# Moving product casts, spills and stores to GpSimd, with four smaller moves, in a fused state-space convolution and gated feed-forward kernel

## The chip, the cores and the metric

The kernel runs on one core of a Trainium2 chip. The metric is the time of one execution on the device, in microseconds (us); lower is better. TensorE is the matmul engine (PE in a profile), VectorE is DVE, ScalarE is ACT, GpSimd is POOL, and SyncE (SP) issues most transfers. SBUF is the memory on the core, PSUM the memory that TensorE writes.

## The reference

The input x has 32 sequences of 64 channels by 1024 places. A convolution along the places comes first: for every channel a kernel of length 1024 is made from 64 complex exponentials, and the input, masked by each sequence's length, is convolved with it.

```python
K = 2.0 * jnp.einsum('hn,hnl->hl', Cs, jnp.exp(P)).real
y = jnp.fft.irfft(u_f * k_f, n=n)[..., :Lq]
y = y + u_m * D[:, None]
return y * mask[:, None, :]
```

Then a gated feed-forward runs over the 2048 rows (32 times 64) of width 1024, with an inner width of 2752. Its three weight matrices are packed in 4 bits, with a scale and a zero point for each group of 128 input rows. The result is added to x.

```python
gate = x2 @ Wg
up = x2 @ Wu
inter = gate * jax.nn.sigmoid(gate) * up
out = (inter @ Wd).astype(jnp.float16)
x = x + out.reshape(B, S, H)
```

## The kernel before, in words

**Convolution.** The 64 channels ("heads") are convolved by matmuls with Toeplitz matrices. A matrix is built by a load that reads the kernel row from device memory (kpad) with an overlapping pattern (`toeplitz`, L488; tiles named t, or borrowed space in w and ihl for the first heads). Each head takes eight steps of three matmuls, since matrix and input are each held as a high and a low half in float16 (`conv_head`, L505, matmuls L521). After two heads VectorE masks the result into y (L533), ScalarE casts its high half into xh (L536), and GpSimd subtracts to get the low half xl (L538). Sixteen heads make one block of 512 columns of the feed-forward's input. There are four blocks.

**Kernel rows.** They are made for eight heads at a time (four at the very start). `tables` (L419) and `factors` (L435) compute exponentials and phases on VectorE and ScalarE; `make_kernel` (L397) multiplies them on TensorE (L401, L403), splits the result (L406 on ScalarE, L407 on VectorE) and stores two halves to kpad (L409). The groups start at heads 0, 4, 8, 16, 24, 32, 40, 48 and 56. The groups of heads 16 and 24 are prepared in `kernel_8` (L841), which is started in the seventh step of the first block's convolution.

**Weights.** `unpack` (L546) loads packed bytes and zero points (z, from the pool "up"), shifts and masks on VectorE (L556), adds zero points on GpSimd (L562) and converts to 8-bit floats on VectorE (L566). There are 22 pieces for gate and up (qgu, qmix) and 8 for the down projection (qdn).

**Chains.** A chain is the sum over the groups of 128 input rows for one PSUM place. After each group the running sum is multiplied by the ratio of scales, on VectorE or ScalarE. The planner keeps one number for the balance, `lag`: work put on VectorE adds its cost, work on ScalarE subtracts, and `rescale` (L581) and `rescale_two` (L601) give the next rescaling to the engine that is behind. `gu_one` (L610) holds gate and up of one block in one chain. `gu_pair` (L632) takes two blocks in one chain: gate chains end in a Silu (L647, tile sg), up chains in the product v (L652). `products` (L589) splits v into two float16 halves: ScalarE casts (L595), GpSimd subtracts (L303, inside `pool_first`). The first block of a pair stays in SBUF (ihl), the second goes through the tile "spill" (one buffer) to device memory (L599). v has one buffer too. `dn_pair` (L667) is the down projection: 22 groups per chain (L677, L678, L680), a residual load (xr, in the two buffers that sg uses), a cast (L696), an addition (L697) and a store (L698). For every second block it loads the spilled products back into ihl (L685).

**Order of work.** The list `items` runs eight stages: 0 and 1 are single chains, four each; 2 is the gate and up pairs of blocks 0 and 1; 3 and 4 the down projection of these blocks; 5 the pairs of blocks 2 and 3; 6 and 7 their down projection. `roll` (L709) goes round the active chains: three in PSUM place "b", and a fourth in place "a" in the stages named wide (1, 2, 5, 6, 7). Beside the chains run side generators at rates: in stage 0 the unpacking and `second` (convolution of block 1), in stages 1 and 2 the unpacking, in stage 2 also `third` (groups 32 and 40), in stages 3 and 4 `fourth` (groups 48 and 56) and `convs` (blocks 2 and 3). RATES holds steps per round. A framework then orders each engine's instructions by priority; `after` and `mark` keep an instruction behind a marked one. Each engine, and each engine's queue of transfers, runs its instructions in order, so a transfer that waits holds up those behind it.

## Time and profile before

| What | us |
|---|---|
| Median of 3 runs (1094.53 to 1096.8) | 1096.46 |
| The profiled execution | 1098.36 |
| Its span, first to last instruction | 1096.1 |
| TensorE busy | 1029.1 |
| VectorE busy | 789.6 |
| ScalarE busy | 775.9 |
| GpSimd busy | 219.3 |
| First convolution matmul | 24.7 |
| First single chain (stage 0) | 66.5 |
| First pair chain (stage 2) | 145.8 |
| First down chain (stage 3) | 412.6 |
| Last convolution matmul | 603.6 |

Busy time of TensorE counts modelled ends of pipelined matmuls. A row of instruction groups gives the line, the engine, the operation, the tiles written and read, the count, busy time and mean, and the idle time before it with what ended it. TensorE's clock can be lowered for a time; the row PEclk gives the granted share.

### The profile page before, as it was taken

How to read it: one execution, taken by the hardware profiler on the slowest of the kernel's cores; microseconds unless marked ns; L12 is line 12 of the kernel's file. 1: busy time of each engine (PE TensorE's matmuls, PEld its weight loads, DVE VectorE, ACT ScalarE, POOL GpSimd, SP SyncE). 2: the span in 40 equal slices, each digit the busy share in tenths (PEclk: the TensorE clock that was granted, in tenths of full speed). 3: DMA queues.
4: the chain of work that ended last, by engine and by line, in shares of the span. 5: the costliest groups of instructions: out<-in, count | busy, mean ns of one | idle time of the engine just before them, and what ended most of it. 6: DMA issues, size and time to landing. Idle time of an engine off the chain costs nothing.

```text
span 1096.1 us, 15375 instructions
## 1 busy us (share of the span) xinstructions
PE 1029.1 (94%) x5834; PEld 515.6 (47%) x5834; DVE 789.6 (72%) x903; ACT 775.9 (71%) x1024; POOL 219.3 (20%) x215
## 2 busy tenths in 40 slices
PE   3889989899999999998998999999999999999996
PEld 3757534344344444554556444444444444444442
DVE  8975578888986667875663767766676667777776
ACT  5636678888887677774663777677777776777775
POOL 0332233443431121113004002111111111002001
PEclk9989999999999999999998999999999999999998
DMA  6866223233200202336665001000000000424202
GB/s 199 288 212 199 85 76 123 83 112 102 73 20 20 79 21 97 130 102 224 211 192 193 1 29 68 20 20 20 20 20 20 20 20 20 144 77 136 86 1 77
DMA packets 55169, 99.73 MB, mean 91 GB/s; under 512 B 9396, under 2 KB 10292, under 8 KB 55096
## 3 DMA queue, kind: packets, MB, share of 16 engines
q1 hardware_dynamic: 54520, 98.73, 27.6%
q8 instruction: 45, 0.74, 0.3%
q14 instruction: 28, 0.23, 0.1%
q10 hardware_dynamic: 576, 0.03, 0.0%
HBM read 78.99 MB, written 19.76 MB: 90 GB/s over the span
## 4 chain that ended last, share of the span: by engine, by line
PE 76%; DVE 9%; DMA 5%; ACT 4%; issue 4%; POOL 1%; SPq 0%; ACTq 0%; DVEq 0%; POOLq 0%
PE chq L639 21%; PE chq L640 20%; PE chq L677 12%; PE chq L678 12%; PE cq L521 6%; PE chq L618 2%; PE chq L619 2%; DMA t<-kpad 2%; DVE chq L584 2%; ACT chq L608 1%; DMA kpad<-kb 1%; DVE chq L604 1%; ACT chq L587 1%; DVE w L566 1%; DVE v L652 1%
## 5 line engine op out<-in xcount | busy, mean ns | idle before, releaser
L639 PE MATMUL chq<-xh,w 128*128 128x512 f16 x1216 | 457.6, 379 | 15.0 <-DVE v L652 8.0
L640 PE MATMUL chq<-xl,w 128*128 128x512 f16 x1216 | 456.0, 379 | 0.0
L587 ACT ACTIVATE chq<-chq,gur 128x1024 f32<-128x1024 f32 x312 | 332.4, 1087 | 106.1 <-PE chq L640 104.9
L584 DVE TENSOR_SCALAR chq<-chq,gur 128x1024 f32<-128x1024 f32 x234 | 299.9, 1290 | 117.9 <-PE chq L640 115.7
L608 ACT ACTIVATE chq<-chq,dnr 128x512 f32<-128x512 f32 x336 | 220.7, 661 | 91.6 <-PE chq L678 86.3
L604 DVE TENSOR_TENSOR chq<-chq,dnr 128x1024 f32<-128x1024 f32 x168 | 206.4, 1232 | 95.7 <-PE chq L678 92.0
L677 PE MATMUL chq<-ihl,wd 128*128 128x512 f16 x672 | 255.1, 380 | 6.9 <-DMA ihl<-spill 2.8
L678 PE MATMUL chq<-ihl,wd 128*128 128x512 f16 x672 | 254.9, 380 | 0.0
L640 PEld LDWEIGHTS <-w 128*128 128x128 fp8e4 x1216 | 118.7, 98 | 163.0 <-issue 26.2
L639 PEld LDWEIGHTS <-w 128*128 128x128 fp8e4 x1216 | 118.7, 98 | 146.5 <-POOL spill L303 2.5
L303 POOL TENSOR_TENSOR ihl<-v,ihl 128x512 f16<-128x512 f32 x42 | 48.9, 1165 | 401.4 <-ACT ihl L595 401.4
L521 PEld LDWEIGHTS <-t 128*128 128x128 f16 x1152 | 85.8, 100 | 44.7 <-DMA t<-kpad 10.2
L678 PEld LDWEIGHTS <-wd 128*128 128x128 fp8e4 x672 | 65.8, 98 | 72.7 <-issue 8.6
L521 PE MATMUL cq<-uh,t 128*128 128x64 f16 (+7 forms) x720 | 93.4, 230 | 6.5 <-DMA t<-kpad 6.2
L677 PEld LDWEIGHTS <-wd 128*128 128x128 fp8e4 x672 | 65.8, 98 | 70.9 <-DMA ihl<-spill 2.9
L538 POOL TENSOR_TENSOR xl<-y,xh 128x512 f16<-128x512 f32 x28 | 34.5, 1235 | 213.8 <-ACT xh L536 178.7
L521 PE MATMUL cq<-ul,t 128*128 128x256 f16 (+3 forms) x360 | 74.3, 230 | 0.1
L652 DVE SCALAR_TENSOR_TENSOR v<-chq,gul,sg 128x1024 f32<-128x1024 f32 x38 | 48.6, 1278 | 15.3 <-PE chq L640 10.4
L608 ACT ACTIVATE chq<-chq,gur 128x512 f32<-128x512 f32 x62 | 40.9, 661 | 20.6 <-PE chq L619 19.6
L618 PE MATMUL chq<-xh,w 128*128 128x512 f16 x128 | 49.2, 390 | 4.2 <-ACT xh L536 3.2
L303 POOL TENSOR_TENSOR spill<-v,spill 128x512 f16<-128x512 f32 x42 | 49.3, 1174 | 8.6 <-ACT spill L595 8.6
L619 PE MATMUL chq<-xl,w 128*128 128x512 f16 x128 | 49.1, 390 | 0.0
(242 smaller groups left out, 721.8 us busy)
## 6 DMA issues: line engine op xcount, KB each, us to landing
t<-kpad SPq DMA_DIRECT2D x48, 512.0 KB, 4.8
spill<-spill SPq DMA_DIRECT2D x42, 256.0 KB, 2.0
ihl<-spill SPq DMA_DIRECT2D x42, 256.0 KB, 2.9
u<-xF SPq DMA_DIRECT2D x12, 512.0 KB, 4.2
xr<-xT SPq DMA_DIRECT2D x12, 512.0 KB, 4.5
out<-xr SPq DMA_DIRECT2D x24, 256.0 KB, 2.6
w<-qgu SPq DMA_DIRECT2D x21, 256.0 KB, 3.9
z<-zc SPq DMA_DIRECT2D x21, 256.0 KB, 3.6
```

The source lines that it names most:

```text
L303: self.nc.gpsimd.tensor_tensor(out, a, b, op)
L521: nc.tensor.matmul(q[:, d:, h % 2, :], t0[:, lw, 128 * d:128 * d + 128], uu[:, 0:8 - d, h % 4, :], start=(d == 0 and k == 0 and h % 2 == 0 ...
L584: self.mark("dve", self.nc.vector.tensor_scalar(q, q, col, None, ALU.mult))
L587: self.mark("act", self.nc.scalar.activation(q, q, AF.Copy, scale=col))
L604: self.mark("dve", self.nc.vector.tensor_tensor(q, q, cols.to_broadcast([128, 2, 512]), ALU.mult))
L608: self.mark("act", self.nc.scalar.activation(q[:, k], q[:, k], AF.Copy, scale=cols[:, k]))
L618: nc.tensor.matmul(q[:, k], lw, xh[:, g, :], start=(g == 0), stop=False, skip_group_check=True)
L619: nc.tensor.matmul(q[:, k], lw, xl[:, g, :], start=False, stop=(g == GH - 1), skip_group_check=True)
L639: nc.tensor.matmul(q[:, b], lw, xh[:, g, :], start=(g == 0), stop=False, skip_group_check=True)
L640: nc.tensor.matmul(q[:, b], lw, xl[:, g, :], start=False, stop=(g == GH - 1), skip_group_check=True)
L677: nc.tensor.matmul(q[:, j], lw, self.ihl[:, g, 0], start=(g == 0), stop=False, skip_group_check=True)
L678: nc.tensor.matmul(q[:, j], lw, self.ihl[:, g, 1], start=False, stop=False, skip_group_check=True)
```

## The change

The same matmuls are issued before and after. What moves:

- Both halves of the product v are made on GpSimd: the 84 casts of L595 become GpSimd copies (`pool_copy`). The planner no longer counts them as ScalarE work.
- GpSimd issues the 42 spills and the 24 output stores of blocks 0 to 2, which SyncE issued.
- The stores of kernel rows for heads under 32 go through ScalarE's queue (before: under 8), six more.
- The conversions of the first three gate and up pieces, two each, run on ScalarE.
- Tables and factors of the group of heads 24 to 31, the fourth group of eight, move from the first convolution into `second`, beside the first chains, and are held behind marked work.
- Unpacking has four z buffers in place of three; down weights come in three pieces per matrix (8, 8 and 6 groups) in place of two of 11.
- From head 32 on, inputs and Toeplitz matrices may be loaded across the border of a block.
- Rates change, and `fourth` steps once for each call where it took two.

```diff
-RATES = {"first": (0.1, 5.0), "second": 0.5, "pairs": 0.45, "third": 0.25,
-         "fourth": 0.9, "convs": 1.6}
+RATES = {"first": (0.1, 5.6), "second": 0.5, "pairs": 0.47, "third": 0.2,
+         "fourth": 1.0, "convs": 1.9}
...
-        self.up = self.up_stack.enter_context(tc.tile_pool(name="up", bufs=3, side="right"))
+        self.up = self.up_stack.enter_context(tc.tile_pool(name="up", bufs=4, side="right"))
...
+    def pool_copy(self, out, a):
+        with self.tc.high_priority(offset=300):
+            self.nc.gpsimd.tensor_copy(out, a)
...
-            (nc.scalar if h0 < 8 else nc.sync).dma_start(
+            (nc.scalar if h0 < 32 else nc.sync).dma_start(
...
-        held = h0 >= 32
+        held = h0 >= 24
...
-                with self.after("dve" if h0 >= 32 else None):
+                with self.after("dve" if h0 >= 24 else None):
...
-            if k // 4 not in self.us and k // 16 == hh // 16:
+            if k // 4 not in self.us and k < 64 and (k // 16 == hh // 16 or hh >= 32):
...
-            if k not in self.t0 and k // 16 == hh // 16 and k in self.known:
+            if k not in self.t0 and (k // 16 == hh // 16 or hh >= 32) and k in self.known:
...
-            with self.after("dve"):
-                nc.vector.tensor_scalar(dst[:, a:b], raw[:, a:b], -64.0, None, ALU.add, saturate=False)
-            self.dve(150 + (b - a) / 2)
+            if act:
+                with self.after("act"):
+                    nc.scalar.activation(dst[:, a:b], raw[:, a:b], AF.Identity, bias=self.cst[:, 108:109], saturate=False)
+            else:
+                with self.after("dve"):
+                    nc.vector.tensor_scalar(dst[:, a:b], raw[:, a:b], -64.0, None, ALU.add, saturate=False)
+                self.dve(150 + (b - a) / 2)
...
-        nc.scalar.copy(hl[:, 0], v)
-        self.act(520)
+        self.pool_copy(hl[:, 0], v)
         self.pool_first(hl[:, 1], v, hl[:, 0], ALU.subtract)
         if b == 1:
-            nc.sync.dma_start(self.spill[i], hl)
+            nc.gpsimd.dma_start(self.spill[i], hl)
...
-            nc.sync.dma_start(self.io["out"][128 * n:128 * n + 128, 512 * blk:512 * blk + 512], xr[:, j])
+            (nc.gpsimd if blk < 3 else nc.sync).dma_start(self.io["out"][128 * n:128 * n + 128, 512 * blk:512 * blk + 512], xr[:, j])
...
-        for k, h0 in ((2, 16), (3, 24)):
-            every(c.tables(kg, h0, 8))
-            every(c.factors(kg, h0, 8, xd[k]))
+        every(c.tables(kg, 16, 8))
+        every(c.factors(kg, 16, 8, xd[2]))
...
-        for _ in range(12):
+        yield from c.tables(kg, 24, 8)
+        for _ in range(3):
+            yield
+        yield from c.factors(kg, 24, 8, xd[3])
+        for _ in range(4):
             yield
         c.make_kernel(kg, 24, 8, "a")
...
-    fourth_it = slowly(fourth(), 2)
+    fourth_it = slowly(fourth(), 1)
```

The rest of the diff gives the down weights and their zero points the layout of the three pieces, and a column of constants for the conversions on ScalarE.

## The prediction

> **What bounds the kernel now.** I read the page first: shares, the forty slices, the chain.
>
> ```profile
> span 1096.1 us, 15375 instructions
> PE 1029.1 (94%) x5834; PEld 515.6 (47%) x5834; DVE 789.6 (72%) x903; ACT 775.9 (71%) x1024; POOL 219.3 (20%) x215
> PEclk9989999999999999999998999999999999999998
> DMA  6866223233200202336665001000000000424202
> PE 76%; DVE 9%; DMA 5%; ACT 4%; issue 4%; POOL 1%; SPq 0%; ACTq 0%; DVEq 0%; POOLq 0%
> ```
>
> TensorE is most of the chain, and the last half of the slices has full clock and little DMA: what can be won lies before slice 23 (620 us). Its 94% is no share of its peak: ends are modelled. So I priced a matmul where nothing interrupts it and compared stretches with that, by the busy time in chosen windows (engine busy time with instruction counts, granted clock, DMA share, GB/s).
>
> ```profile
> 62.00:66.50 4.50, 1.24 (x18) 0.81 (x19) 3.80 (x7) 1.28 (x3) 3.41 (x5) 0.80 0.39 129
> 66.50:72.00 5.50, 5.50 (x15) 1.97 (x15) 2.70 (x5) 1.55 (x3) 0.19 (x1) 0.54 1.00 299
> 118.00:145.80 27.80, 27.75 (x128) 12.20 (x126) 21.43 (x23) 22.14 (x35) 4.51 (x6) 1.00 0.05 19
> 173.00:310.00 137.00, 125.39 (x564) 54.79 (x563) 120.46 (x187) 115.60 (x125) 59.28 (x65) 1.00 0.30 96
> 310.00:412.00 102.00, 101.42 (x491) 45.51 (x490) 73.09 (x68) 74.92 (x82) 18.81 (x17) 1.00 0.10 32
> 588.00:595.00 7.00, 2.97 (x31) 2.08 (x32) 0.69 (x1) 0.62 (x1) 3.17 (x3) 0.91 0.79 253
> 595.00:604.00 9.00, 9.00 (x98) 8.12 (x97) 0.94 (x2) 0.62 (x1) 1.16 (x1) 0.69 0.32 113
> 604.00:945.00 341.00, 340.93 (x1572) 153.43 (x1571) 240.22 (x191) 247.80 (x276) 52.16 (x46) 1.00 0.07 26
> ```
>
> From 118 to 145.8 us, 128 matmuls of 512 columns take 27.8 us: 0.217 us each. From 604 to 945 it is 341/1572 = 0.217 again, with both vector engines idle 30% of the time. That stretch and the 139 us after it are TensorE alone; no edit to another engine can shorten them. From 173 to 310, 564 x 0.217 = 122.4 us of 137: 14.6 us lost, with VectorE 88% and ScalarE 84% busy. Around 62 and 588 the clock is low and TensorE waits. The chain of waits, and the SyncE queue by time, say why at 588:
>
> ```profile
> 578.95 3.46 DMA out<-xr
> 582.95 4.96 DMA t<-kpad
> 587.95 1.36 PE cq L521 x15
> 589.31 5.19 DMA t<-kpad
> 594.55 9.10 PE cq L521 x96
> ```
> ```profile
> 585.22 4.04 SPq L698 DMA_DIRECT2D out<-xr  x4
> 589.31 8.69 SPq L499 DMA_DIRECT2D t<-kpad  x4
> ```
>
> The four stores of the output hold SyncE from 585.22 to 589.26, each until its POOL addition is done, and the load of the next convolution matrix stands behind them.
>
> **What the skill says.** The Trainium skill, GPSIMD Engine Reference, section 4.1, has GpSimd about half as fast as VectorE with two inputs and "1-input is roughly line-rate"; section 3.1 gives 2.6 cycles an element for two. The trace agrees on two: the subtraction of L303 (128x512) takes 1165 ns. DMA: Bandwidth & Descriptors, "Latency and other measured facts", prices the first byte of a GpSimd transfer at 1 us against 0.6 us for SyncE or ScalarE, and its anatomy section has 2.0 us plus bytes/436 GB/s; no run here has a GpSimd transfer. SBUF — State Buffer, "Who interferes with whom": two-port VectorE modes lock GpSimd out, and GpSimd's descriptors with it. The unpacking conversion L566 averages 829 ns, with single ones from 0.63 to 1.65 us, as such a lock would make it. TensorE: Matmul & The Clock Gate, Part 1: after a pause the array runs at half rate until it has been busy about 3.4 us. The trace agrees: after the gap at 62 us matmuls start 0.43 us apart until 71.5.
>
> **The change, part by part.** Sums are against the profiled run (span 1096.1, run 1098.36), in us saved.
>
> (a) Both product parts on POOL. ScalarE loses 84 casts (L595, 612 to 616 ns), 51.6 us; POOL gains 84 copies. Bounds of a copy: 0.44 us (512 elements at line rate, an estimate from the page) and 1.17 us (the two-input row); I take 0.75, so 63 us, which lies in POOL's 80% idle time. Only what falls in 173 to 310 is worth time: nine pairs end there, 18 x 0.614 = 11.1 us less for ScalarE, and the planner's lag spreads it over both engines. Divided by two: 5.5. Bounds 0 (TensorE's own waits stay) and 11 (all is critical). After 310 ScalarE's idle time covers it. Against it: POOL now holds v longer. By the timeline v is held 3.0 us from the end of L652 to the last subtraction, and free for 3.1 us before the next close pair, from 310 on for 0.8 to 3.7. With POOL: 2 x 0.75 + 2 x 1.165 = 3.8, plus up to 1 of a transfer's issue ahead of it. What queues behind the late L652 is VectorE's rescaling and, on TensorE, the chain that wants that PSUM place: -1 (0 to -4; the copies at 1.17 make 4.7).
>
> (b) Spills and output stores on POOL: 66 transfers, each 1 us of issue (estimate from the page; 0.4, SyncE's issue, to 2.6), 66 us of POOL time behind its own results. SyncE loses 66 waits, 440.5 us behind L303 and some 100 behind the additions. The stage's end gains: the longest wait for t<-kpad, 4.5, plus half rate afterwards: 96 matmuls took 9.1 where two heads at 53.5 us (48 in 3.22) make it 6.4, so 2.7. Together 7.2; I take 6.5, since these loads still wait for their three buffers (4 to 7.2). At 508 the load ihl<-spill was issued behind two stores: TensorE waited 2.8, then eight starts 0.43 apart lost 1.7; 4.5, of which I take 3.5 (0 to 4.5). Spill of the second block's single chains, 147.8 to 151.9: lands 4.04 after issue; POOL's would need 2.6 (estimate, 256 KB): 1 (-1 to 2).
>
> (c) h0 < 32 stores of kernel rows on ScalarE: six issues of 0.3 to 0.7 us leave SyncE, where group 8's last was issued at 34.47, group 16's at 63.60 behind a u load waiting until 61.46. TensorE waits 3.0 at 44.76; VectorE's half is ready only at 33.74, so the issue moves 0.7, and the landing (6.2) shortens as it leaves the row of 512 KB loads: 2 (0 to 3). On ScalarE the second issue waits for VectorE ahead of a y cast; nobody waits for that cast there.
>
> (d) First three conversions on ScalarE (6 of 1.13 us, estimate from ScalarE: Activation LUTs, "What ACT_TABLE_LOAD costs", 0.28 us + 0.833 ns an element; VectorE loses 6 x 0.83 to 1.2), and group 24's tables and factors (some 13 VectorE operations, 6.5 to 7 us) out of the first convolution. VectorE is 100% busy from 50 to 62 and TensorE waits for L533 there: 1.69 + 0.49 = 2.2 saved (0 to 2.2). At the end of that convolution, group 16's half row L407 ran at 63.17 in the old order; in the new one it stands before the last two y, and the next convolution's first matmuls come ahead of the first chain. Old: 61.5 to 72.4 for 16 matmuls and a kernel group (4.4 of work), 6.5 lost. New: the load lands an estimated 2 to 4 after the end, plus 2 of half rate: 2.5 saved (0 to 5).
>
> (e) Group 24 within the first chains: its 7 us meet VectorE at 16.3 of 30 busy (82 to 112). The new TensorE order puts 88 conv and 36 chain matmuls, 13 us plus the cold start, ahead of it; the VectorE chain up to e1 is about 20 us: costs 0 to 2. Waits there of 0.8 (L566) and 2.0 (t<-kpad at 116) ease: net 1.5 (-2 to 2.8).
>
> (f) Early loads across convolution blocks, four z buffers, rates, dn pieces in three (four more L556, about 2 us of VectorE in its fullest stretch): the loads are in (b); -2 for the pieces and for waits in new places that I can't name (-6 to +1).
>
> Sum: 5.5 - 1 + 6.5 + 3.5 + 1 + 2 + 2.2 + 2.5 + 1.5 - 2 = 21.7. The profiled run becomes 1098.4 - 21.7 = 1076.7. The median of the runs shown is 1.9 under the profiled one: 1075. Every low end together is 9 lost, every high end 39 saved; neither is likely.
>
> **Rivals.**
>
> Queue only (0.20): POOL's longer hold eats what ScalarE gives up. For it: L652 already ends 8.0 us of TensorE's waits at L639. Then the 5.5 goes, and half of (c) to (e), 4.1: 12 saved, 1084.
>
> All waits (0.13): the 14.6 lost to 310 mostly vanish, since both engines drop below the point at which TensorE waits: 33 saved, 1063. Against it: 236 of 274 us of engine time falls only to about 226.
>
> No change (0.04): new waits match the gains; 1096.
>
> Slower (0.13): POOL becomes the pace. Copies at 1.17, a transfer's issue at 2.6, one unpack piece at 0.75 and a lock of 0.8 ahead give a hold of 2.3 + 2.3 + 2.6 + 0.75 + 0.8 = 8.8 against 6.1 free. 2.7 us late at all 17 pairs before 430 is 46; if three quarters reach TensorE, 34 against 22 saved: 1108. It decides from a hold of about 7.8, where 17 x 1.7 x 0.75 meets the 22. Against it: VectorE's PSUM rescales show no two-port speed (1290 ns for 1024), so most POOL work would run unlocked.
>
> **How the numbers follow.** Main case 0.50, 1066 to 1084. 80% range: leave out most of the slower case, the no-change case's upper half and the tail under 1062: 1062 to 1094. Faster 0.50 + 0.20 + 0.13 = 0.83; same (within 0.2%, about 2 us, as fine as this kernel can be measured) 0.04; slower 0.13.
>
> **What would show it.** Right: no gap over 2 us before L521 near 590 and full clock after it; VectorE and ScalarE both under 85% in the pairs before 310; L533 no longer ending waits near 60. POOL near 350 us busy. Wrong: L652 waiting on POOL; waits of L521 for t<-kpad at the first chains; TensorE waiting for group 24's e1; copies over 1.2 us.

## The result: no change that can be measured

The changed kernel takes 1097.07 us (median of 20 runs, 1093.66 to 1100.91), the kernel before 1095.99 us (20 runs, 1094.52 to 1097.66) in the same comparison. The ratio is 1.001, with a 95% interval of 1.0 to 1.0019. The prediction had 1075 and 83% for faster: it was wrong. Of its cases it is the one given 0.04, in which new waits match the gains.

The page of the profile after, the lines that answer to those shown of before:

```profile
span 1096.3 us, 15389 instructions
PE 1026.1 (94%) x5834; PEld 512.9 (47%) x5834; DVE 764.4 (70%) x879; ACT 761.8 (69%) x969; POOL 304.9 (28%) x365
...
PEclk9989999998999999999999999999999999999998
DMA  6866223222200201335754101000000000424202
...
PE 72%; DVE 8%; POOL 3%; DMA 3%; ACT 2%; issue 2%; SPq 0%; DVEq 0%; POOLq 0%; ACTq 0%
```

VectorE and ScalarE gave up 25 and 14 us, 39 together where 51.6 us of casts alone left ScalarE, and GpSimd took 86. The span is the same, and GpSimd is 3% of the chain where it was 1%. The same eight windows as before (busy us and instruction counts of TensorE, its weight loads, VectorE, ScalarE and GpSimd, then granted clock, DMA share, GB/s) say where time went:

```profile
62.00:66.50 4.50, 2.77 (x12) 1.64 (x12) 0.00 (x0) 0.00 (x0) 0.00 (x0) 0.50 1.01 315
66.50:72.00 5.50, 5.50 (x36) 2.85 (x35) 4.40 (x8) 3.06 (x5) 0.00 (x0) 0.82 0.70 259
118.00:145.80 27.80, 26.90 (x124) 12.00 (x123) 19.62 (x19) 21.73 (x34) 8.55 (x10) 1.00 0.08 25
173.00:310.00 137.00, 122.03 (x534) 52.87 (x532) 111.27 (x164) 104.08 (x102) 68.24 (x87) 0.96 0.26 87
310.00:412.00 102.00, 98.08 (x472) 43.90 (x472) 76.96 (x80) 70.76 (x74) 33.83 (x41) 1.00 0.11 35
588.00:595.00 7.00, 7.00 (x60) 4.33 (x59) 4.36 (x5) 4.75 (x8) 3.66 (x4) 1.00 0.37 116
595.00:604.00 9.00, 9.00 (x91) 6.17 (x89) 5.79 (x6) 4.26 (x7) 5.36 (x7) 1.00 0.53 184
604.00:945.00 341.00, 340.41 (x1575) 153.64 (x1574) 227.93 (x180) 239.19 (x246) 93.45 (x117) 1.00 0.08 29
```

Two rows carry the result. At 588 to 604 TensorE now works without a gap and at full clock (before: 2.97 us busy of the first 7, clock 0.91 and 0.69). From 173 to 310 it issues 534 matmuls where it issued 564: 30 x 0.217 us = 6.5 us lost, although VectorE fell from 120.5 to 111.3 us and ScalarE from 115.6 to 104.1. From 310 to 412 it is 19 matmuls, 4.1 us. Not all of the loss is waiting: from 173 to 310 the granted clock is 0.96 where it was 1.00.

By the first matmul of each kind in the timelines, the stages stand as follows (us; "pair stage" is from here on the stage of blocks 0 and 1, from the first pair chain to the first down chain, and "stretch" is the time from that down chain to the last convolution matmul):

| | before | after |
|---|---|---|
| first single chain | 66.5 | 64.7 |
| first pair chain | 145.8 | 143.0 |
| first down chain | 412.6 | 421.1 |
| last convolution matmul | 603.5 | 603.4 |
| pair stage | 266.8 | 278.1 |
| stretch | 190.9 | 182.3 |

The pair stage lost 11.3 us, the stretch won 8.6, and 2.8 were ahead at the start. Each of the first two is made of idle time of TensorE and of time at a lowered clock. In the pair stage the idle time went from 15.1 to 21.2 us, and the clock, full throughout before the change, was at half (granted share 0.50) for 13.7 us (from 147.0 for 3.4, from 211.8 for 3.4, from 246.0 for 6.8). TensorE was busy for 11.7 of these 13.7 us, so by an estimate from these figures the half clock cost about 5.9 us, as much as the added idle time. In the stretch the idle time went from 11.4 to 8.1 us and the half clock from 10.2 to 3.4. The view of waits (what TensorE waited for: us in all, times, longest), from 140 to 425 us, names the loss. Before:

```profile
PE chq L639 <- DVE v L652: 8.0, 7, 1.8
```

After (L650 is the old L639, L663 the old L652):

```profile
PE chq L650 <- DVE v L663: 15.6, 6, 5.5
```

A new chain waits for its PSUM place until VectorE has made the product v from what stands there. The longest such wait ends at 212.42; the next ones end at 247.27 and 311.88. As gaps, that is as time between the starts of two matmuls beyond the length of one at full rate, they are 5.7, 5.0 and 3.0 us, and the experiments speak of gaps in this sense. The first two are where the clock fell to half at 211.8 and 246.0. TensorE's timeline there (start, us, what, and in brackets the idle time before it and what ended it):

```profile
206.52 0.38 PE L651 MATMUL chq<-xl,w 128*128 128x512 f16 x1
212.42 0.59 PE L650 MATMUL chq<-xh,w 128*128 128x512 f16 x1 [5.51 <-DVE v L663]
```

VectorE's timeline between this product and the one before it:

```profile
200.16 1.27 DVE L663 SCALAR_TENSOR_TENSOR v<-chq,gul,sg 128x1024 f32<-128x1024 f32 x1
...
203.02 1.44 DVE L562 TENSOR_SCALAR w<-w,cst 128x1024 uint16<-128x1024 uint16 x1
204.38 1.17 DVE L91 SCALAR_TENSOR_TENSOR t<-t 128x64 f32<-128x64 f32 x1
205.47 0.96 DVE L562 TENSOR_SCALAR w<-w,cst 128x1024 uint16<-128x1024 uint16 x1
206.36 2.75 DVE L91 SCALAR_TENSOR_TENSOR t<-t 128x64 f32<-128x64 f32 x2
209.03 0.68 DVE L576 TENSOR_SCALAR w<-w 128x1024 fp8e4<-128x1024 uint8 x1
209.63 0.47 DVE L91 SCALAR_TENSOR_TENSOR t<-t 128x64 f32<-128x64 f32 x2
...
211.09 1.27 DVE L663 SCALAR_TENSOR_TENSOR v<-chq,gul,sg 128x1024 f32<-128x1024 f32 x1
```

And GpSimd's in the same time:

```profile
201.50 1.00 POOL L309 CAST ihl<-v 128x512 f16<-128x512 f32 x1 [3.39 <-DVE v L663]
202.45 0.61 POOL L309 CAST spill<-v 128x512 f16<-128x512 f32 x1
203.02 1.15 POOL L305 TENSOR_TENSOR ihl<-v,ihl 128x512 f16<-128x512 f32 x1
204.14 1.33 POOL L305 TENSOR_TENSOR spill<-v,spill 128x512 f16<-128x512 f32 x1
205.43 0.72 POOL L568 TENSOR_TENSOR w<-w,z 128x256 int32<-128x256 int32 x1
206.10 0.56 POOL L610 DMA_DIRECT2D spill<-spill  x1
206.68 2.08 POOL L568 TENSOR_TENSOR w<-w,z 128x256 int32<-128x256 int32 x3
```

GpSimd works without a break from 201.50 to 208.76: two copies, two subtractions, the issue of the spill, four unpack additions. VectorE, meanwhile, does not wait for data; its instructions take long. The small L91 on 64 elements, 0.22 us when GpSimd is still (209.63, two in 0.47), takes 1.17 and then 2.49 (the first of the two at 206.36; it ends 0.09 us after GpSimd's last addition). The shift L562, 0.47 undisturbed, takes 1.44 and 0.96. The Silu that the product needs was done at 205.40; the product started at 211.09, because all of this stands ahead of it in VectorE's order. Over 150 to 410 us VectorE's instructions took 31.0 us more than their undisturbed lengths (an estimate, with the tenth percentile of each operation and shape for undisturbed); before the change it was 19.7. The rescaling L596, which reads and writes PSUM, is not stretched: it takes 1291 ns on average, before it took 1290.

At 63 us, a new wait stands where old ones were (TensorE, 30 to 70 us): 4.4 us for a load ahead of the first chain, which the prediction had listed as a sign against it. The two waits for L533 that step d was to end, 1.69 us at 58.4 and 0.49 at 62.1, are gone. In all, TensorE's waits from the first convolution matmul to the first pair chain add up to 11.9 us where they were 13.2: most of them moved. Those for loads:

```profile
PE cq L527 <- DMA t<-kpad: 7.1, 2, 4.4
```

SyncE's queue near 590 (SPq rows: start, us in the queue, how many) no longer holds a store; two loads of the convolution matrix still wait there for 4.92 us, but TensorE has other matmuls meanwhile. The wait near 510 did not go: for 2.8 us at 511.9 before (`ihl<-spill`) there are now two for the same load, 2.0 at 520.7 and 2.3 at 531.3. The queue:

```profile
584.15 4.28 SPq L696 DMA_DIRECT2D ihl<-spill  x2
589.12 4.92 SPq L505 DMA_DIRECT2D t<-kpad  x2
```

### The profile page after: what moved, and what is told of

It is laid out like the page before. It is cut to its first block, busy times and chain, and to the rows that moved or that the text cites. A ratio compares the mean times of both kernels' runs of the same rounds, so it can differ in the third digit from the quotient of the medians.

```text
span 1096.3 us, 15389 instructions
## 1 busy us (share of the span) xinstructions
PE 1026.1 (94%) x5834; PEld 512.9 (47%) x5834; DVE 764.4 (70%) x879; ACT 761.8 (69%) x969; POOL 304.9 (28%) x365
## 4 chain that ended last, share of the span: by engine, by line
PE 72%; DVE 8%; POOL 3%; DMA 3%; ACT 2%; issue 2%; SPq 0%; DVEq 0%; POOLq 0%; ACTq 0%
PE chq L650 21%; PE chq L651 20%; PE chq L688 12%; PE chq L689 12%; PE cq L527 4%; DVE chq L596 2%; PE chq L629 1%; PE chq L630 1%; DVE v L663 1%; POOL w L568 1%; DMA out<-xr 1%; ACT chq L619 1%; POOL spill L305 1%; DMA spill<-spill 1%; ACT sg L658 1%
## 5 line engine op out<-in xcount | busy, mean ns | idle before, releaser
L650 PE MATMUL chq<-xh,w 128*128 128x512 f16 x1216 | 462.7, 382 | 21.2 <-DVE v L663 15.6
L651 PE MATMUL chq<-xl,w 128*128 128x512 f16 x1216 | 461.5, 382 | 0.6 <-DVE xl L544 0.6
L599 ACT ACTIVATE chq<-chq,gur 128x1024 f32<-128x1024 f32 x333 | 353.2, 1086 | 147.7 <-PE chq L651 147.1
L596 DVE TENSOR_SCALAR chq<-chq,gur 128x1024 f32<-128x1024 f32 x213 | 273.6, 1291 | 135.1 <-PE chq L651 130.7
L650 PEld LDWEIGHTS <-w 128*128 128x128 fp8e4 x1216 | 119.3, 98 | 145.6 <-issue 3.7
L309 POOL CAST ihl<-v 128x512 f16<-128x512 f32 x42 | 28.0, 666 | 332.1 <-DVE v L663 250.8
L527 PE MATMUL cq<-uh,t 128*128 128x64 f16 (+6 forms) x720 | 92.9, 227 | 6.0 <-DMA t<-kpad 6.0
L663 DVE SCALAR_TENSOR_TENSOR v<-chq,gul,sg 128x1024 f32<-128x1024 f32 x38 | 48.5, 1277 | 17.6 <-PE chq L651 13.0
L658 ACT ACTIVATE sg<-chq,gul 128x1024 f32<-128x1024 f32 x38 | 42.3, 1112 | 11.9 <-PE chq L651 11.8
L708 POOL TENSOR_TENSOR xr<-xr,o 128x512 f32<-128x512 f32 x24 | 28.4, 1186 | 79.3 <-ACT o L707 78.1
L629 PE MATMUL chq<-xh,w 128*128 128x512 f16 x128 | 49.4, 389 | 0.2 <-ACT chq L619 0.2
```

What stands on the lines that cost most here:

```text
L527: nc.tensor.matmul(q[:, d:, h % 2, :], t0[:, lw, 128 * d:128 * d + 128], uu[:, 0:8 - d, h % 4, :], start=(d == 0 and k == 0 and h % 2 == 0 ...
L596: self.mark("dve", self.nc.vector.tensor_scalar(q, q, col, None, ALU.mult))
L599: self.mark("act", self.nc.scalar.activation(q, q, AF.Copy, scale=col))
L629: nc.tensor.matmul(q[:, k], lw, xh[:, g, :], start=(g == 0), stop=False, skip_group_check=True)
L650: nc.tensor.matmul(q[:, b], lw, xh[:, g, :], start=(g == 0), stop=False, skip_group_check=True)
L651: nc.tensor.matmul(q[:, b], lw, xl[:, g, :], start=False, stop=(g == GH - 1), skip_group_check=True)
```

## The experiments

All times are medians; a ratio is against the kernel before, measured on the same chip, with its 95% interval. The sets were measured on different chips, where the kernel before had medians of 1095.99 to 1097.2 us, so a difference between medians of two sets carries about 1 us of this; the ratios don't. Pair stage, stretch and waits are of the one profiled execution of each kernel.

### First set: one part undone, or one part alone

**Casts back on ScalarE**, the rest of the change kept:

```diff
-        self.pool_copy(hl[:, 0], v)
+        nc.scalar.copy(hl[:, 0], v)
+        self.act(520)
```

> The changed kernel with one part undone: the high half of v is cast on ScalarE again, and counted in lag. Theory 1 (GpSimd's product copies stand ahead of the unpack additions, so VectorE's conversions, and the product behind them in its order, come late): the pair stage of blocks 0 and 1, 278 us in the changed kernel, goes back to 267 to 270, the three gaps of TensorE of 5.7, 5.0 and 3.0 us go, and the time is 1085 to 1089 (ratio 0.990 to 0.993 to the kernel before). Rival (rates, four z buffers and pieces in three moved the unpacking into a worse place, whoever casts): the stage stays at 275 to 282 and the time at 1094 to 1101.

Measured: 1090.54 us, ratio 0.9939 (0.9919 to 0.9959); pair stage 270.6. Theory 1 in its main point, a little outside its ranges (by 1.5 us in time): without the copies the changed kernel is 6.5 us faster, 7.8 by the ratios, and 7.5 of the 11.3 us return in the pair stage, where TensorE's idle time is back at 15.8 us and the half clock at 6.8.

**Copies alone**, on the kernel before:

```diff
-        nc.scalar.copy(hl[:, 0], v)
-        self.act(520)
+        self.pool_copy(hl[:, 0], v)
```

> The kernel before with one part of the change: only the high half of v is copied on GpSimd, and lag no longer counts it. Theory 1: the pair stage of blocks 0 and 1 grows from 267 to 272 to 278 us and the time is 1101 to 1107 (ratio 1.005 to 1.010). Rival (the copies are harmless or help, as the prediction had it): 1090 to 1096, the stage at 261 to 267.

Measured: 1096.04 us, ratio 0.999 (0.9982 to 0.9998); pair stage 274.0. The stage is as theory 1 had it (7.2 us longer), the time is not. The profile gives 2.3 us back in the stretch (188.6) and 2.8 after it (480.4 us from the last convolution matmul to the end of the last matmul, 483.2 before). No load or store has moved here, and yet the gap of 4.03 us at 594.55 is three waits of 1.9, 0.9 and 1.4, with the clock full: that gap seems to depend on when the work before it comes, and part of the loss may come back by it; how was not followed. Its first pair chain is at 143.0, but that is where some runs of unchanged code have it (below), so it is no gain. The waits of the three kernels for v, from 140 to 425 us: copies alone first,

```profile
PE chq L642 <- DVE v L655: 12.5, 5, 4.2
```

then the change with the casts back:

```profile
PE chq L651 <- DVE v L664: 7.9, 5, 2.6
```

**Old rates beside the pair chains**, in the changed kernel:

```diff
-RATES = {"first": (0.1, 5.6), "second": 0.5, "pairs": 0.47, "third": 0.2,
+RATES = {"first": (0.1, 5.6), "second": 0.5, "pairs": 0.45, "third": 0.25,
```

> The changed kernel with the two rates that act beside the pair chains put back (pairs 0.45, third 0.25). Theory 1: the copies remain, so the stage stays at 273 to 281 us and the time at 1092 to 1101. Rival (the rates): the stage goes to 267 to 270, the time to 1086 to 1090.

Measured: 1101.69 us, ratio 1.0039 (1.0024 to 1.0053); pair stage 281.4. The rival falls: putting the old rates back costs the changed kernel 4.6 us, 3.2 by the ratios.

**Stores and spills on GpSimd alone**, on the kernel before:

```diff
-            nc.sync.dma_start(self.spill[i], hl)
+            nc.gpsimd.dma_start(self.spill[i], hl)
...
-            nc.sync.dma_start(self.io["out"][...], xr[:, j])
+            (nc.gpsimd if blk < 3 else nc.sync).dma_start(self.io["out"][...], xr[:, j])
```

> The kernel before with one part of the change: GpSimd issues the spills and the output stores of blocks 0 to 2. Theory 1 with the prediction's part b: the gap of TensorE near 590 goes and the clock stays full there, the stretch from the first down chain to the last convolution shrinks from 191 us by 6 to 8.5, and the time is 1087 to 1090 (ratio 0.992 to 0.994). Rival (the loads across block borders and the rate of the convolutions took that gap away, not the stores): the stretch shrinks by under 3, the time is 1092 to 1097.

Measured: 1097.55 us, ratio 1.0003 (0.9992 to 1.0013); stretch 188.4, pair stage 268.9. The rival holds: the stretch is 2.5 us shorter, the pair stage 2.1 longer. With the stores gone from SyncE the loads still wait, now for matmuls to free their three buffers (SyncE's wait for L521 is 9.8 us between 560 and 605): the one long gap near 590 becomes several shorter ones (TensorE, 585 to 602 us):

```profile
PE cq L521 <- DMA t<-kpad: 6.4, 4, 2.7
```

### Second set: what shortened the stretch, and what holds the product

**The convolution side alone**, on the kernel before. No transfer moves to GpSimd:

```diff
-         "fourth": 0.9, "convs": 1.6}
+         "fourth": 1.0, "convs": 1.9}
...
-            if k // 4 not in self.us and k // 16 == hh // 16:
+            if k // 4 not in self.us and k < 64 and (k // 16 == hh // 16 or hh >= 32):
...
-            if k not in self.t0 and k // 16 == hh // 16 and k in self.known:
+            if k not in self.t0 and (k // 16 == hh // 16 or hh >= 32) and k in self.known:
...
-    fourth_it = slowly(fourth(), 2)
+    fourth_it = slowly(fourth(), 1)
```

> The kernel before with one part of the change: inputs and Toeplitz matrices loaded across the border of a block from head 32 on, the rates 1.0 and 1.9, one step a call for the last kernel groups. GpSimd issues no transfer. Theory 2 (this, not the stores, shortened the down stages): the stretch from the first down chain to the last convolution goes from 191 us to 181 to 185, the time to 1088 to 1091. Rival (the stores on GpSimd are needed with it): the stretch stays at 186 to 192 and the time at 1093 to 1098.

Measured: 1087.16 us, ratio 0.9912 (0.9891 to 0.9933); stretch 178.8, 12.1 us shorter, more than in the changed kernel. Theory 2 holds, and both values are better than its ranges. The last heads are convolved earlier, among the chains' matmuls: TensorE's idle time in the stretch falls from 11.4 to 5.8 us, and the time at half clock from 10.2 to none. The last 16.5 us up to the last convolution matmul:

```profile
572.00:588.50 16.50, 16.42 (x153) 10.67 (x151) 9.75 (x9) 9.78 (x16) 7.38 (x7) 1.00 0.47 160
```

TensorE is busy throughout and at full clock, with the stores still on SyncE. The same run settles another point: up to the first pair chain this kernel has the instructions of the kernel before, and it gets there at 142.8 us, the kernel before in its profile at 145.8. So 3 us at that place is what one execution differs from another, and the 2.8 us of the changed kernel there are not shown to be a gain. Which does more, the rates, the early loads or the smaller steps of `fourth`, was not separated.

**Two buffers for v**, in the changed kernel (here and below, one of three places where v is made):

```diff
-            v = self.fw.tile([128, 2, 512], F32, name="v", bufs=1)
+            v = self.fw.tile([128, 2, 512], F32, name="v", bufs=2)
```

> The changed kernel with two buffers for the product v in place of one; VectorE's order stays the same. Theory A (the unpack additions stand behind product copies and subtractions in GpSimd's order, so the conversions come late, and the products behind them in VectorE's order): v's buffer is not what the product waits for, the pair stage of blocks 0 and 1 stays at 275 to 281 us and the time at 1094 to 1100. Rival B, the prediction's second half of step a (GpSimd holds v longer, the next product waits for the buffer): the stage goes to 267 to 272, the time to 1086 to 1091.

Measured: 1094.53 us, ratio 0.9982 (0.9972 to 0.9991); pair stage 275.8. In A's range: the second buffer is worth 2.5 us, and the waits for v stay at 15.0.

**Conversions one step later**, in the changed kernel (and the rates of unpacking raised to 0.62 and 0.59):

```diff
         yield
+        if not act:
+            yield
         for a, b in zip(cuts, cuts[1:]):
```

> The changed kernel with one more step between GpSimd's unpack additions and VectorE's conversions of the same piece (the rates of unpacking raised from 0.5 and 0.47 to 0.62 and 0.59, since a piece now takes five steps for four). Theory A: VectorE finds its data ready, the waits of TensorE for the product v fall from 16 us to 7 to 10, the stage goes to 268 to 273 us, the time to 1087 to 1092. Rival B: the waits stay at 14 to 18, the stage at 275 to 282, the time at 1094 to 1101.

Measured: 1097.88 us, ratio 1.0002 (0.9992 to 1.0013); pair stage 276.9, waits for v 13.9. Theory A fell as it stood. Near 210 the conversions now have their data when VectorE comes to them; the gap is still 5.3 us: the small operations and the shifts ahead of the product are stretched as shown above, one of them again to 2.5 us. The higher rates were not tried by themselves, here or below.

**Casts back and conversions later**, together (rates 0.62 and 0.59 again):

```diff
-        self.pool_copy(hl[:, 0], v)
+        nc.scalar.copy(hl[:, 0], v)
+        self.act(520)
...
         yield
+        if not act:
+            yield
```

> The changed kernel with the casts on ScalarE again and the conversions one step later. Theory A: conversions that come early for GpSimd cost something in this order too: the stage goes from 270.6 us to 265 to 268, the time from 1090.5 to 1085 to 1088. Rival (with the casts on ScalarE GpSimd's additions are early enough): 270 to 273 and 1089 to 1093.

Measured: 1089.9 us, ratio 0.9939 (0.9921 to 0.9957); pair stage 267.1. The stage is A's; the time is the rival's and not below that with the casts back alone (1090.54) by more than its uncertainty. Inconclusive for the time.

### Third set: the small operations, the planner, and the combinations

**Without the coefficient operations** of heads 32 to 63, in the changed kernel:

```diff
-        coefficients = head_coefficients(nc, nc.vector, co, take, c.prm, c.cst[:, 66:67], 32, 32)
-        while True:
...
+        with c.after("dve"):
+            for k in ("na", "wh", "wl"):
+                nc.vector.tensor_copy(co[k][:, 32:64], co[k][:, 0:32])
+            nc.vector.tensor_copy(co["ab"][:, :, 32:64], co["ab"][:, :, 0:32])
+        for _ in range(14):
```

> The changed kernel without VectorE's coefficient operations for heads 32 to 63 (some 70 small ones beside the pair chains); four copies take the coefficients of heads 0 to 31 in their place, so the convolution of blocks 2 and 3 is not the reference's. Unpacking, copies and the planner's numbers stay. Theory 3 (VectorE's operations that share SBUF's port with GpSimd stand still while GpSimd works back to back, and these small ones stand ahead of the products): TensorE's gaps of 5.7 and 5.0 us near 212 and 247 fall below 1.5, its waits for v from 16 to under 7 us, the pair stage of blocks 0 and 1 from 278 to 265 to 271. Theory A (VectorE waits for GpSimd's additions with its conversions): the unpacking is the same, so both gaps stay at 3 or more, the stage at 273 to 279.

Measured: 1095.08 us, ratio 0.9985 (0.9976 to 0.9994); pair stage 276.4, gaps of 4.9 and 4.2 us left. Theory 3 alone fell too. Here a conversion stands ahead of the product: it waits 2.84 us for additions that come after GpSimd's copies and subtractions, and then takes 3.16 us where it takes 0.68 undisturbed, ending 0.56 us after the last instruction of GpSimd's run.

**The planner's count put back**, copies still on GpSimd:

```diff
         self.pool_copy(hl[:, 0], v)
+        self.act(520)
```

> The changed kernel with 520 ns counted for ScalarE in lag at each product, as before the change, while GpSimd still makes the copy: only the share of rescalings between VectorE and ScalarE moves. Theory 3 (GpSimd's copies hold VectorE up): the stage stays at 275 to 281 us, the time at 1094 to 1100. Rival C (the planner, no longer counting the casts, gives the rescalings to the wrong engine): the stage goes to 268 to 272, the time to 1087 to 1091.

Measured: 1103.39 us, ratio 1.0057 (1.004 to 1.0074); pair stage 282.2. Rival C falls: the count is not what costs; put back without the cast it harms, by 6.3 us.

**The convolution side with stores and spills on GpSimd** (the edits of the two experiments with each alone, together; here the part that is added to the convolution side):

```diff
-            nc.sync.dma_start(self.spill[i], hl)
+            nc.gpsimd.dma_start(self.spill[i], hl)
...
-            nc.sync.dma_start(self.io["out"][...], xr[:, j])
+            (nc.gpsimd if blk < 3 else nc.sync).dma_start(self.io["out"][...], xr[:, j])
```

> The kernel before with the convolution side of the change, and spills and output stores on GpSimd. If the prediction's step b is right in its sign: stretch of the down chains to the last convolution 176 to 178 (178.8 without), time 1084 to 1087. If the stores take GpSimd's time from the additions and the unpacking: stage of pairs 268 to 270, stretch 179 to 182, time 1087 to 1091.

Measured: 1090.52 us, ratio 0.9945 (0.9924 to 0.9965); pair stage 270.5, stretch 181.8. On top of the convolution side the transfers on GpSimd cost 3.4 us, near the uncertainty of the difference. Both places are longer, the pair stage by 3.6 us and the stretch by 3.0, but these are two single executions, 1084.12 us there and 1094.13 here, and overstate it. Each spill's issue, 0.59 us on average, is time of GpSimd between its subtractions and the unpack additions.

**The convolution side with later conversions and two buffers for v**, casts on ScalarE, spills and stores on SyncE:

```diff
-RATES = {"first": (0.1, 5.0), "second": 0.5, "pairs": 0.45, "third": 0.25,
+RATES = {"first": (0.1, 5.0), "second": 0.62, "pairs": 0.56, "third": 0.25,
...
-            v = self.fw.tile([128, 2, 512], F32, name="v", bufs=1)
+            v = self.fw.tile([128, 2, 512], F32, name="v", bufs=2)
...
         yield
+        yield
         for a, b in zip(cuts, cuts[1:]):
```

> The kernel before with the convolution side of the change (1087.2 us by itself), conversions one step later (rates 0.62 and 0.56) and two buffers for v, casts on ScalarE, spills and stores on SyncE. If the waits for v in the pair stage (9.1 us) are late conversions and the buffer: stage 261 to 265, time 1081 to 1085. If they are VectorE's own load: stage 266 to 269, time 1086 to 1089.

Measured: 1077.81 us, ratio 0.982 (0.9801 to 0.9839); pair stage 260.6. It beats both kernels by about 19 us, more than expected. Its window beside the changed kernel's 534 matmuls:

```profile
173.00:310.00 137.00, 129.81 (x581) 56.30 (x580) 124.51 (x190) 118.59 (x128) 58.26 (x64) 1.00 0.31 94
```

VectorE is at 91% and ScalarE at 87% of this window, more than in either kernel, and TensorE gets 47 matmuls more than in the changed one, at full clock. Full engines are not what stops it.

### Fourth set: is it one wall?

**Later conversions and no coefficient operations together**, in the changed kernel (rates 0.62 and 0.59):

```diff
         yield
+        if not act:
+            yield
...
-        coefficients = head_coefficients(nc, nc.vector, co, take, c.prm, c.cst[:, 66:67], 32, 32)
...
+                nc.vector.tensor_copy(co[k][:, 32:64], co[k][:, 0:32])
```

> The changed kernel with the conversions one step later and without the coefficient operations of heads 32 to 63 (those of heads 0 to 31 are copied, so the convolution of blocks 2 and 3 is not the reference's). Theory W (GpSimd's unbroken run of copies, subtractions and additions is a wall: a conversion waits at it for its data, a small operation for the port, and either alone keeps the product behind it): with both gone the gaps near 212 and 247 (5.3 and 4.3 with one, 4.9 and 4.2 with the other) fall below 2, the waits for v below 9 us, the stage to 266 to 272. Rival D (the product is late for something else): gaps of 3.5 or more stay, the stage at 274 to 278.

Measured: 1092.83 us, ratio 0.9968 (0.9955 to 0.9981); pair stage 273.6, gaps of 4.5 and 3.1 us. Theory W missed its range, and the stage came out 0.4 us under D's. VectorE's timeline shows why: with the small operations gone, a conversion was next to the product again, even one step later.

```profile
198.56 1.58 DVE L562 TENSOR_SCALAR w<-w,cst 128x1024 uint16<-128x1024 uint16 x2
202.98 3.76 DVE L578 TENSOR_SCALAR w<-w 128x1024 fp8e4<-128x1024 uint8 x2 [2.84 <-POOL w L568]
206.66 1.27 DVE L665 SCALAR_TENSOR_TENSOR v<-chq,gul,sg 128x1024 f32<-128x1024 f32 x1
```

**The same, conversions two steps later** (rates 0.74 and 0.71), so that a conversion with older data stands there:

```diff
         if not act:
             yield
+            yield
```

> As h1 (changed kernel without the coefficient operations of heads 32 to 63, so blocks 2 and 3 of the convolution are not the reference's), the conversions two steps later for one (rates 0.74 and 0.71). In VectorE's order a conversion whose additions were issued before the first product of a close pair now stands between the two products. Theory W: no conversion waits there for data; a lock of the port remains for the length of one copy or subtraction; the gaps of 4.5 and 3.1 us near 208 and 241 fall below 1.5, the waits for v from 13.1 to below 8 us, the stage from 273.6 to 266 to 270. Rival D: gaps of 3 or more stay at the close pairs, the stage at 272 to 276.

Measured: 1088.98 us, ratio 0.9938 (0.992 to 0.9957); pair stage 268.2, in theory W's range. The gaps at the close pair near 200 and 207 are 1.9 and 1.4 us, one just above the 1.5 expected. VectorE's timeline:

```profile
200.72 2.73 DVE L579 TENSOR_SCALAR w<-w 128x1024 fp8e4<-128x1024 uint8 x3
205.61 1.28 DVE L666 SCALAR_TENSOR_TENSOR v<-chq,gul,sg 128x1024 f32<-128x1024 f32 x1 [2.15 <-POOL spill L305]
```

Nothing stands ahead of the product now, and before a pair's product it now waits for what the prediction had feared: the one buffer of v, 2.15 us. The waits for v are still 11.0 us in all (expected under 8): a gap of 4.7 us near 328 is the old picture, conversions behind a GpSimd run from 317.55 to 325.89.

**Copies on GpSimd in the best version**:

```diff
-        nc.scalar.copy(hl[:, 0], v)
-        self.act(520)
+        self.pool_copy(hl[:, 0], v)
```

> The version of 1077.8 us (kernel before with the convolution side, later conversions, two buffers for v) with one edit: GpSimd copies the high half, lag doesn't count it. Theory W: the conversions no longer wait, but the shift of the unpacking and the coefficient operations still stand still for GpSimd's longer run, so the pair stage goes from 260.6 to 264 to 270, the time to 1081 to 1088. Rival E (copies did harm only through one buffer of v and early conversions together): 258 to 262 and 1075 to 1079.

Measured: 1086.6 us, ratio 0.9912 (0.9894 to 0.993); pair stage 271.5. The copies cost 8.8 us here, 10.1 by the ratios, and 10.9 in the pair stage, though v has two buffers and the conversions are late. The stage's idle time goes from 8.1 to 15.4 us, and the clock, full without the copies, is at half for 13.7 us. Waits for v from 140 to 425 us, against 2.3 without the copies:

```profile
PE chq L643 <- DVE v L656: 12.7, 6, 3.5
```

**One buffer for v in the best version**:

```diff
-            v = self.fw.tile([128, 2, 512], F32, name="v", bufs=2)
+            v = self.fw.tile([128, 2, 512], F32, name="v", bufs=1)
```

> The version of 1077.8 us with one buffer for v. If the later conversions are the gain: 1077 to 1080, stage 260 to 263. If the second buffer is half of it: 1081 to 1085, stage 263 to 265.

Measured: 1083.1 us, ratio 0.9874 (0.9855 to 0.9893); pair stage 263.3. So the later conversions with their rates are worth 4.1 us there (1087.16 to 1083.1) and the second buffer 5.3.

**The change without its GpSimd parts**, with later conversions (rates 0.62 and 0.59) and two buffers for v:

```diff
-        self.pool_copy(hl[:, 0], v)
+        nc.scalar.copy(hl[:, 0], v)
+        self.act(520)
...
-            nc.gpsimd.dma_start(self.spill[i], hl)
+            nc.sync.dma_start(self.spill[i], hl)
...
-            (nc.gpsimd if blk < 3 else nc.sync).dma_start(self.io["out"][...], xr[:, j])
+            nc.sync.dma_start(self.io["out"][...], xr[:, j])
...
-            v = self.fw.tile([128, 2, 512], F32, name="v", bufs=1)
+            v = self.fw.tile([128, 2, 512], F32, name="v", bufs=2)
...
         yield
+        if not act:
+            yield
```

> The changed kernel with the casts on ScalarE and all spills and stores on SyncE again, conversions one step later, two buffers for v. If steps c to e, the rates and the pieces in three are worth what the prediction gave them (some 7 us): 1069 to 1074. If they are worth nothing: 1076 to 1081. If the pieces and rates harm the pair stage: 1081 to 1087, the stage at 264 to 268.

Measured: 1082.44 us, ratio 0.9872 (0.9852 to 0.9892); pair stage 263.6. Steps c to e, the four z buffers, the pieces in three and the other rates, together, cost 4.6 us beside the best version, which lacks them. The stage is just under the range expected for harm, the time in it.

**The best version with the conversions two steps later** (rates 0.74 and 0.67):

```diff
         yield
         yield
+        yield
         for a, b in zip(cuts, cuts[1:]):
```

> The version of 1077.8 us with the conversions two steps later (rates 0.74 and 0.67). Its waits for v are 3.1 us in the pair stage, so at most 2 are left to win: 1075 to 1079 if the rates do no harm, up to 1083 if they do.

Measured: 1078.21 us, ratio 0.9838 (0.9815 to 0.986): nothing more to win by it.

## Why the prediction was wrong

Measured kernels make a ladder from before to after, by ratio to the kernel before: with the convolution side 0.9912; with stores and spills on GpSimd too 0.9945; with everything but the copies 0.9939; with the copies, the whole change, 1.001. In medians the steps are -9.9, +3.4, 0.0 and +6.5 us, in ratios about -9.6, +3.6, -0.7 and +7.8. Each step is uncertain by 2 to 3 us either way: the first and the last are clear of that, the second is near it, the third is not to be told from nothing.

**Step a failed, and decided the result.** It put 63 us of copies into "POOL's 80% idle time" and took 5.5 less 1 as the gain; it is a loss of 6.5. The copies' length was nearly right (0.64 to 0.67 us on average, 0.75 taken). The GPSIMD Engine Reference of the Trainium skill, section 4.1, calls one-input work roughly line-rate; an undisturbed copy takes 0.61 us, 0.17 over the estimate of 0.44 made from it and far from the 1.17 of two inputs. Wrong was the averaging of idle time. GpSimd's work is not spread over the stage: at each product it comes in one run, and the copies lengthen that run just where the unpacking of the next weights is due on VectorE, ahead of the next product. The prediction asked what queues behind the late L652, but not what stands ahead of it and waits for GpSimd. It also had the other half in its hands. It cited SBUF — State Buffer, "Who interferes with whom", for VectorE locking GpSimd out. The same section says that whoever issues first gets the shared ports and the other "fully blocks". The trace agrees, with GpSimd as the holder: 2.49 us for an instruction of 0.22, ending 0.09 us after GpSimd's last addition. And step a had no term for the clock, which the prediction did price at 590 and at 508: about half of the pair stage's loss is time at half clock.

That the copies cost 6.5 and 8.8 us in the whole kernel is shown in two settings, and 7.2 to 10.9 in the pair stage in three; on the kernel before alone the time did not move, since about 5 us came back later. The way in which they do it is shown for the gap near 207, which stayed when one or the other thing stood before the product and shrank to 1.4 us when neither did; for the others it is read from traces. Not tried were copies that stand behind the unpack additions in GpSimd's order, in place of ahead of them.

**The term "POOL holds v longer", -1**, was about right in size: a second buffer gives 2.5 us in the changed kernel, within the 0 to 4 allowed. Its place was wrong. VectorE waits for the buffer not before the products of the pairs, at which the prediction looked, but at the edges of the stage: before the products of two late single chains 1.73 and 2.33 us (0.81 and 1.85 before the change), and before that of the mixed chain at 432 us 2.36 (1.17 before). In the best version, where ScalarE casts, the second buffer gives 5.3 us, and the waits of VectorE that it ends lie outside the pairs' products there too. v is held 3.5 to 4.3 us up to 310 us (3.8 foreseen), and 5.3 at most after that, so the rival "slower", which needed 7.8, had the wrong mechanism.

**Step b, +11, failed in its cause.** The gap near 590 went and the clock stayed full, both listed as signs that the step was right; but the stores alone are worth nothing (1.0003), and with the convolution side they cost some 3.4. The wait at 508, +3.5, did not end either: with stores and spills on GpSimd alone TensorE waits for `ihl<-spill` 1.3 and 2.1 us where it waited 2.8, in the changed kernel 2.0 and 2.3; with the convolution side alone and the stores on SyncE it is 1.4. And the spill, +1, lands no earlier: 2.3 us after its issue begins, as the median of all 42, where SyncE's took 2.0; the 4.04 at 147.8 was one transfer. Step b noted that the loads "still wait for their three buffers" and took 6.5 all the same. The gain belonged to **step f**, which had put the early loads down to b and the rates among the costs: the convolution side is worth 9.9. A sign that two causes would both produce does not tell them apart.

**Steps c to e, +8.2, show no gain.** The first pair chain comes at 143.0, and unchanged code has it between 142.8 and 145.8. The waits for L533 went, as step d had it, but others came in their place. The wait at 44.76 that was to shrink by 2 is 2.7 us long for 3.0, and at the end of the first convolution the load of the next matrix came 4.4 us after TensorE had run out of matmuls (2 to 4 estimated); VectorE, ScalarE and GpSimd did nothing from 62 to 66.5 either, by the window's row. With the rates, buffers and pieces of step f these steps cost 4.6 us beside the best version, and 0.0 in the ladder, where the conversions come early and v has one buffer; their shares were not separated.

**What else held or not.** The last 480 us are TensorE's alone and did not move (483.2 and 483.4 us). VectorE and ScalarE fell to 81% and 76% from 173 to 310, under the 85% named as a sign of success, and it was none. GpSimd is 305 us busy where near 350 was named: an issue takes it 0.58 us on average, not the 1 estimated. The half rate after the gap at 62 us lasted from 64.7 to 71.5 before the change, 6.8 us and not about 3.4; other stretches in these traces last 3.4. The six conversions on ScalarE take 1.13 to 1.15 us, as estimated.

## What to carry to other kernels

Before moving work to an idle engine, look at when that engine's runs fall and who waits for its results or shares its ports then; a share of idle time says nothing of it. Read, from the order of each queue, what stands ahead of the instruction that the bound engine waits for. And test each part alone when one symptom has two causes: here the part costed at a loss was the whole gain. Last, price a wait together with the lowered clock that follows it.

## What the runs showed of the hardware that was not expected

- A VectorE instruction with operands in SBUF can be held through several GpSimd instructions, not one: 3.16 us for a conversion of 0.68 and 2.49 us for an operation of 0.22, each across the rest of a spill's issue and three additions of 0.72 that followed each other at once.
- GpSimd issues a transfer in 0.56 us (stores) or 0.59 (spills) of its own time on average, at most 0.97. The spill of 256 KB lands 2.3 us after the issue begins; from SyncE, before the change, it landed after 2.0 (medians).
- Two executions of the same instructions reached the first pair chain 3 us apart (142.8 and 145.8 us), so a gain of that size cannot be read from one profile.
